# Negative mean, second sum and z on ScalarE, in a two-layer graph network scheduled by a planner

## The chip, the cores and the metric

The kernel runs on one core of one Trainium2 chip. The core has five engines that run side by side, each through its own queue: TensorE (PE in the profile), VectorE (DVE), ScalarE (ACT), GpSimd (POOL) and SyncE (SP), which here only issues DMAs. What is measured is device time in microseconds (us) of one launch; less is better.

## The reference, cut to what matters

There are 64 batches of 256 tokens with 512 features (float32). The first layer is masked attention with 8 heads, the second a graph attention with scores from two vectors; each is added to its input and normalized over the features, without scale or shift.

```python
def _layernorm(x, axis=-1, eps=1e-5):
    m = jnp.mean(x, axis=axis, keepdims=True)
    v = jnp.var(x, axis=axis, keepdims=True)
    return (x - m) / jnp.sqrt(v + eps)

# layer 0: out = softmax(q k^T / 8 + (1 - adj) * -1e9) v, per head
x = _layernorm(x + out @ Wo + bo)
# layer 1
h = x @ W
e = leaky_relu(s1[:, :, None] + s2[:, None, :], 0.2) * adj     # s1 = h a1, s2 = h a2
x = _layernorm(x + elu(softmax(e, axis=2) @ h + beta * h))
```

## The kernel before, in words

**Tiling.** A batch's tokens lie on the 128 partitions in two tiles (NT = 2), with 512 features along the free dimension. Two batches make a pair (function pair, L620): they share the products for q, k and v. There are 32 pairs, m = 0 to 31; the two batches of a pair are s = 0 and s = 1. Every product with a weight is done by project (L435), a seven-product scheme in place of eight: each product goes into a PSUM tile, some are copied out by ScalarE (L495 and, with a bias for q and k, L498) and others added on by VectorE (L504, L954). The copies matter for order: the fourth product of a project adds onto the PSUM tile of the first, so it has to wait until ScalarE has copied the first out; likewise the fifth or sixth (into ps_cross) waits for the copy of the second.

**Steps of a batch.** scores (four products in pairs of heads, L782), mask and exponential (L789, L791), sums (denominators, L805), mix (attention times v, L749), o (output product added to X, L954), the first norm, two dot products of X with vectors on VectorE (L977), logits (the graph scores, L987 to L1028), attention (transposed through DRAM, L1030 to L1050), spread (attention times X, L1106), u (times W, L1111), finish (L716: ELU and the second norm, and the output's DMA).

**norm (L584).** For two tiles of X it takes the sum of each (ScalarE, Identity with an accumulator output; L592), multiplies it by -1/512 on VectorE (mean, L598), squares X plus this negative mean on ScalarE with a sum (L592 again), takes a power of -1/2 on GpSimd (L603 to L605), and applies scale and bias on ScalarE (L609). For the second norm the sum of X comes with the last VectorE operation of finish (L724, accum_out), and is given to norm, which then leaves out its Identity.

**z (L1006).** The graph score of a query and a key is a sum of one number per partition (sv) and one per column (row). The column's numbers are a row that is written to DRAM (line, L1001) and read back to all partitions (row, L1003); z is row plus sv on VectorE. After it come leaky relu (VectorE, L1012), the mask (GpSimd, L1015), the maximum (VectorE, L1017), the exponential (ScalarE, L1020), the division (VectorE, L1026).

**The planner (class Plan, L62).** Every operation is entered with its engine, an assumed duration in ns, what it reads and writes, and a mode. place (L127) simulates the engines with these durations and writes out one order, in which the instructions are issued; each engine then goes through its instructions in that order. An operation of GpSimd, and one of VectorE with the mode "two", takes a common "port" in this simulation and has to wait for it. Of the operations that could start, the one with the earliest start is placed; at equal start the engine that comes first in the table LAG (L73). The lag of each engine is the assumed time until another engine sees its result.

TensorE's operations have a fixed order: take_turn (L613) gives each step of pair m the round m + LATER[step], and inside a round the place in ROUND. The last pairs follow FINISH instead, and for the last 70 TensorE operations (OPEN) the plan chooses freely. "x", "logits" and "attention" are turns without TensorE work: they only fix when their buffers are claimed and what may start after them.

Of the kernel before, what the change touches and what calls it, by code (L numbers as in the profile page):

```python
# [11 lines left out]
AF = mybir.ActivationFunctionType  # L12
ALU = mybir.AluOpType
# [6 lines left out]
ALPHA = 0.2  # L20
NEG = -1000000000.0

ROUND = ("x", "v", "spread1", "scores20", "scores10", "scores30", "scores00", "o1", "q", "logits1", "u1", "sums0",
         "mix0", "scores11", "scores21", "scores01", "scores31", "attention0", "k", "spread0", "o0", "mix1",
         "logits0", "sums1", "u0", "attention1")

LATER = {"scores20": 0, "x": -1, "scores10": 0, "v": 0, "logits0": 0, "spread1": 2, "o1": 1, "q": -1, "u1": 2,
         "sums0": 0, "mix0": 0, "scores11": 0, "scores01": 0, "attention0": 1, "attention1": 1, "scores31": 0,
         "scores21": 0, "k": -1, "logits1": 1, "spread0": 1, "o0": 0, "u0": 1, "sums1": 0, "mix1": 0, "scores00": 0,
         "scores30": 0}  # L30

FINISH = (("scores00", 0), ("scores20", 0), ("scores10", 0), ("v", 0), ("attention1", 1), ("spread1", 2),
          ("scores30", 0), ("logits1", 1), ("o1", 1), ("sums0", 0), ("u1", 2), ("attention0", 1), ("mix0", 0),
          ("scores11", 0), ("spread0", 1), ("u1", 0), ("logits0", 0), ("o0", 0), ("sums1", 0), ("spread1", 1),
          ("mix1", 0), ("attention1", 0), ("spread0", 0), ("scores21", 0), ("attention0", 0), ("u0", 0),
          ("logits1", 0), ("o1", 0), ("u1", 1), ("scores31", 0), ("u0", 1), ("scores01", 0), ("spread1", 0))
SAFE = 1e15


# [22 lines left out]
class Plan:  # L62
# [7 lines left out]

    LAG = {"PE": 260.0, "DVE": 70.0, "ACT": 70.0, "POOL": 90.0, "SP": 4200.0}  # L73
    KEPT = {"PE": 0.0, "DVE": 80.0, "ACT": 95.0, "POOL": 40.0, "SP": 0.0}
    AFTER = {"PE": 0.0, "DVE": 30.0, "ACT": 30.0, "POOL": 80.0}
    SWITCH = {None: 100.0, "rows": 200.0, "columns": 100.0, "sums": 100.0, "one": 100.0}
    AGAIN = 100.0
    LATER = 15000.0
    OPEN = 70
# [47 lines left out]
    def place(self):  # L127
# [22 lines left out]
        for n, o in enumerate(ops):  # L150
            if due[n] is None:
                due[n] = max((due[d] + (self.LATER if ops[d][0] == "PE" else ops[d][1]) for d in o[3]), default=0.0)

# [90 lines left out]
def gnn_two_layers(ctx: ExitStack, tc: tile.TileContext, x, adj, Wq, bq, Wk, bk, Wv, bv, Wo, bo, W, a, beta, out):  # L244
    nc = tc.nc
    B, N, D = x.shape
# [24 lines left out]
    plan = Plan(slots)  # L271
    stay = []
    A = slice(None)
# [7 lines left out]
    def st(n, name):  # L281
        return sb("st", [n], name)
# [298 lines left out]
    for sv in spare:  # L581
        plan.op("POOL", 100, lambda sv=sv: nc.gpsimd.memset(sv[A], 0.0), [], [sv])

    def norm(X, ts, given=None):  # L584

        n = len(ts)
        mean, sq, rs, nm = (st(n, name) for name in ("mean", "sq", "rs", "nmr"))
        sums = given or st(n, "sum")

        def total(i, t, func, to, bias):  # L590
            junk = sb("half", [D], "junk")
            plan.op("ACT", 815 if bias else 725, lambda: nc.scalar.activation(  # L592
                junk[A], X[:, t, :], func, bias=mean[:, i:i + 1] if bias else 0.0, accum_out=to[:, i:i + 1]),
                [(X, (t, 0)), (X, (t, 1))] + ([mean] if bias else []), [junk, (to, i)])

        for i, t in enumerate(ts if given is None else ()):
            total(i, t, AF.Identity, sums, False)
        plan.op("DVE", 170, lambda: nc.vector.tensor_scalar(mean[A], sums[A], -1.0 / D, None, ALU.mult), [sums], [mean])  # L598
        for i, t in enumerate(ts):
            total(i, t, AF.Square, sq, True)  # L600

        def rsqrt():
            nc.gpsimd.tensor_scalar(rs[A], sq[A], 1.0 / D, EPS, ALU.mult, ALU.add)  # L603
            nc.gpsimd.tensor_tensor(rs[A], rs[A], neg_half[A].to_broadcast([P, n]), ALU.pow)
            nc.gpsimd.tensor_tensor(nm[A], mean[A], rs[A], ALU.mult)  # L605

        plan.op("POOL", 1250, rsqrt, [sq, mean], [rs, nm])
        for i, t in enumerate(ts):
            plan.op("ACT", 810, lambda i=i, t=t: nc.scalar.activation(  # L609
                X[:, t, :], X[:, t, :], AF.Identity, bias=nm[:, i:i + 1], scale=rs[:, i:i + 1]),  # L610
                [nm, rs], [(X, (t, 0)), (X, (t, 1))])

    def take_turn(m, what):  # L613
        at_end = (what, B // 2 - 1 - m) if m is not None else None
        if at_end in FINISH:
            plan.turn = (B // 2 + 1, FINISH.index(at_end))
        else:
            plan.turn = ((m or 0) + LATER[what], ROUND.index(what))

    def pair(m, at, general=False):  # L620
# [56 lines left out]
        if m == 0:  # L677
# [11 lines left out]
            left["v"] = weight_sums(wv_sb, "sv_sb", "POOL")  # L689
            plan.turn = (0, ROUND.index("x"))  # L690
            left["o"] = residual_bias()
# [11 lines left out]
    def batch(m, s, qT, kT, V, dram, general):  # L703
# [4 lines left out]
        X = sb("x", [NT, D], f"x_{b}")  # L708
# [4 lines left out]
        def tokens(t):  # L713
            return [(X, (t, 0)), (X, (t, 1))]

        def finish(ts, us, u, mode):  # L716

            sums = st(len(ts), "sum")
            for t in ts:
                m = sb("half", [D], "m")  # L720
                plan.op("ACT", 620, lambda t=t, m=m: nc.scalar.activation(m[A], u(t), AF.Exp), us(t), [m])
                plan.op("DVE", 685, lambda t=t: nc.vector.scalar_tensor_tensor(  # L722
                    X[:, t, :], u(t), 0.0, X[:, t, :], op0=ALU.max, op1=ALU.add), us(t), tokens(t), mode=mode)
                plan.op("DVE", 770, lambda t=t, m=m: nc.vector.scalar_tensor_tensor(  # L724
                    X[:, t, :], m[A], 1.0, X[:, t, :], op0=ALU.min, op1=ALU.add,
                    accum_out=sums[:, t - ts[0]:t - ts[0] + 1]), [m], tokens(t) + [(sums, t - ts[0])], mode="two")
            norm(X, ts, sums)
            for t in ts:
                plan.op("SP", 455, lambda t=t: nc.sync.dma_start(dram(out, s)[:, t, :], X[:, t, :]), tokens(t), [],
                        lag=2300)  # L730
# [238 lines left out]
        if b == 0:  # L969
            plan.turn = (0, ROUND.index("k"))  # L970
            left["w"] = second_layer_constants()

        sv = spare[(b or 0) % len(spare)]
        for t in range(NT):
            for i in range(2):
                junk = sb("half", [D], "junk")
                plan.op("DVE", 770, lambda t=t, i=i, junk=junk: nc.vector.scalar_tensor_tensor(  # L977
                    junk[A], X[:, t, :], 1.0, wa_sb[:, i, :], op0=ALU.mult, op1=ALU.mult,
                    accum_out=sv[:, t, 1 - i:2 - i]), tokens(t) + [(wa_sb, i)], [junk, (sv, (i, t))],
                    mode="two")  # L980


        z, e = sb("half", [NT, N], "z"), sb("half", [NT, N], "e")
# [4 lines left out]
        if near:  # L988
            row = ps([N], "tr_s")
# [6 lines left out]
        else:  # L996
            line, row = Buf(dram_pool, "line", [N], "line"), sb("half", [N], "row")
# [5 lines left out]
            plan.op("SP", 430, lambda: nc.sync.dma_start(row[A], row_on_all(line[A], 0, N)), [line], [row], lag=3800)  # L1003
        nm1, sm1, rc1 = st(NT, "nm1"), st(NT, "sm1"), st(NT, "rc1")
        for t in range(NT):
            plan.op("DVE", 430, lambda t=t: nc.vector.tensor_scalar(  # L1006
                z[:, t, :], row[A], sv[:, t, 1:2], None, ALU.add), [row, (sv, (0, t))], [(z, t)], mode="two")

        for ts in ((0, 1), (1, 2)) if near else ((0, 2),):
            ts, k = slice(*ts), ts[1] - ts[0]  # L1010
# [71 lines left out]
        sums = [(lambda i=i: S[:, i]) for i in range(4)]  # L1082
# [39 lines left out]
    fine, row, least = st(2, "fine"), ps([P], "row"), st(1, "least")  # L1122
# [17 lines left out]
    with tc.If(again != 0):  # L1140
# [3 lines left out]
        with tc.For_i(0, B, 2) as i:  # L1144
            for tile_ in stay:
                tile_.parts = {}
            plan = Plan({**slots, "half": slots["half"] - 1})
# [34 lines left out]
```

## Time and profile before

| what | us |
|---|---|
| median of 3 runs | 2713.54 (2713.28 to 2713.59) |
| the profiled execution, own time | 2716.73 |
| its span, first to last instruction | 2714.9 |
| a round in the middle, from one mix0 to the next | 83.70 |
| PE busy, in that round | 82.25 |
| DVE, ACT, POOL busy in that round | 70.1, 44.6, 51.9 |
| the last PE product to the end of the span | 12.2 |

The profiled execution is 0.12% above the median, so sums over its trace are compared with 2716.73, and the difference is carried over to the median. The busy time of TensorE rests on modelled ends, but a gap between its products is a gap. Between 100 and 2590 us the rounds repeat. The clock of TensorE is full except for 3.5 us near 2641 us.

### The profile page before, as it was taken

How to read it: one execution, taken by the hardware profiler on the slowest of the kernel's cores; microseconds unless marked ns; L12 is line 12 of the kernel's file. 1: busy time of each engine (PE TensorE's matmuls, PEld its weight loads, DVE VectorE, ACT ScalarE, POOL GpSimd, SP SyncE). 2: the span in 40 equal slices, each digit the busy share in tenths (PEclk: the TensorE clock that was granted, in tenths of full speed). 3: DMA queues.
4: the chain of work that ended last, by engine and by line, in shares of the span. 5: the costliest groups of instructions: out<-in, count | busy, mean ns of one | idle time of the engine just before them, and what ended most of it. 6: DMA issues, size and time to landing. Idle time of an engine off the chain costs nothing.

```text
span 2714.9 us, 45841 instructions
## 1 busy us (share of the span) xinstructions
PE 2650.2 (98%) x15037; PEld 2283.0 (84%) x15037; DVE 2256.1 (83%) x4439; ACT 1427.2 (53%) x3201; POOL 1663.8 (61%) x2255
## 2 busy tenths in 40 slices
PE   9999999999999999999999999999999999999997
PEld 7888888888888888888888888888888888888886
DVE  6888888888888888988889888888888888888977
ACT  3455555555554555545555555555455554555555
POOL 5665575655666656656557565575665666656654
PEclk9999999999999999999999999999999999999999
DMA  8444353443444443434435344343444443443321
GB/s 252 95 103 121 101 128 90 116 112 108 121 107 107 106 120 109 122 93 114 119 103 133 86 114 119 105 124 97 116 106 114 115 114 101 108 124 100 98 57 55
DMA packets 583084, 300.70 MB, mean 111 GB/s; under 512 B 409400, under 2 KB 513848, under 8 KB 582840
## 3 DMA queue, kind: packets, MB, share of 16 engines
q1 hardware_dynamic: 582712, 297.68, 41.8%
q8 instruction: 123, 2.02, 0.3%
q14 instruction: 121, 0.99, 0.1%
q0 software_dynamic: 128, 0.01, 0.0%
HBM read 245.11 MB, written 52.48 MB: 110 GB/s over the span
## 4 chain that ended last, share of the span: by engine, by line
PE 87%; DVE 9%; ACT 3%; issue 1%; DMA 0%; POOL 0%; SPq 0%; DVEq 0%; POOLq 0%; ACTq 0%
PE ps_chain L455 29%; PE ps_cross L455 21%; PE ps_sc L782 8%; PE ps_pv L759 8%; PE ps_fourth L455 7%; PE ps_pair L455 7%; PE ps_second L455 5%; DVE mean L598 3%; DVE flip L800 2%; ACT junk L592 2%; DVE part L801 1%; DVE x L954 1%; ACT qT L498 1%; DMA wq_sb<-in_L_gnn_Wq_dram 0%; PE ps_den L809 0%
## 5 line engine op out<-in xcount | busy, mean ns | idle before, releaser
L794 POOL TENSOR_TENSOR both<-pT 128x256 f32<-128x256 f32 x504 | 379.3, 776 | 11.0 <-ACT pT L791 11.0
L791 ACT ACTIVATE pT<-pT 128x512 f32<-128x512 f32 x512 | 309.9, 629 | 106.0 <-DVE pT L789 105.5
L789 DVE TENSOR_TENSOR pT<-ps_sc,maskT_sb 128x512 f32<-128x512 f32 x512 | 317.8, 682 | 13.6 <-PE ps_sc L782 11.6
L1086 POOL TENSOR_TENSOR X_sums<-x 128x256 f32<-128x256 f32 x126 | 126.3, 1018 | 256.2 <-DVE x L722 204.9
L977 DVE SCALAR_TENSOR_TENSOR junk<-x,wa_sb 128x512 f32<-128x512 f32 x256 | 225.1, 914 | 50.6 <-ACT x L609 49.6
L1015 POOL TENSOR_TENSOR e<-e,adj_sb 128x512 f32<-128x512 f32 (+1 forms) x66 | 82.6, 1252 | 290.0 <-DVE e L1012 287.6
L592 ACT ACTIVATE junk<-x 128x512 f32<-128x512 f32 x128 | 80.1, 626 | 322.9 <-DVE x L954 313.7
L592 ACT ACTIVATE junk<-x,mean 128x512 f32<-128x512 f32 x256 | 182.8, 716 | 120.5 <-DVE mean L598 120.5
L782 PE MATMUL ps_sc<-qT,kT 64*128 64x256 f32 x2048 | 238.9, 383 | 0.0
L759 PE MATMUL ps_pv<-pT,v 128*64 128x256 f32 x2048 | 238.4, 382 | 0.0
L609 ACT ACTIVATE x<-x,nmr,rs 128x512 f32<-128x512 f32 x256 | 197.6, 808 | 58.2 <-POOL nmr L605 55.6
L782 PEld LDWEIGHTS ps_sc<-qT,kT 64*128 64x128 f32 x2048 | 192.6, 187 | 37.0 <-issue 13.3
L759 PEld LDWEIGHTS ps_pv<-pT,v 128*64 128x64 f32 x2048 | 175.6, 137 | 44.6 <-issue 11.0
L603 POOL TENSOR_SCALAR rs<-sq 128x2 f32<-128x2 f32 (+1 forms) x130 | 34.8, 268 | 281.9 <-ACT junk L592 276.7
L800 DVE STREAM_TRANSPOSE flip<-both 128x512 f32<-128x512 f32 x252 | 176.6, 701 | 8.2 <-DVE part L801 0.5
L801 DVE TENSOR_REDUCE part<-flip 128x16 f32<-128x512 f32 x252 | 168.8, 670 | 0.3
L455 PE MATMUL ps_cross<-xT,wq_sums 128*128 128x256 f32 x496 | 120.2, 385 | 43.0 <-ACT qT L498 43.0
L743 POOL TENSOR_TENSOR x<-x,res_sb 128x512 f32<-128x512 f32 x128 | 161.0, 1280 | 0.9 <-DMA x<-in_x_dram 0.9
L455 PEld LDWEIGHTS ps_cross<-xT,wq_sums 128*128 128x128 f32 x496 | 91.8, 190 | 65.9 <-ACT qT L498 54.6
L598 DVE TENSOR_SCALAR mean<-sum 128x2 f32<-128x2 f32 (+1 forms) x130 | 112.0, 862 | 34.8 <-ACT junk L592 34.6
L954 DVE TENSOR_TENSOR x<-x,ps_chain 128x256 f32<-128x256 f32 x252 | 101.5, 413 | 40.2 <-PE ps_chain L455 37.0
L455 PE MATMUL ps_chain<-so_sb,oS 128*128 128x256 f32 x504 | 129.7, 380 | 0.0
(248 smaller groups left out, 7179.8 us busy)
## 6 DMA issues: line engine op xcount, KB each, us to landing
x<-in_x_dram SPq DMA_DIRECT2D x64, 512.0 KB, 7.9
out_dram<-x SPq DMA_DIRECT2D x128, 256.0 KB, 3.1
inv_all<-rows SPq DMA_DIRECT2D x126, 256.0 KB, 3.8
xin<-in_x_dram SPq DMA_DIRECT2D x248, 128.0 KB, 3.0
wq_sums<-wq_sums SPq DMA_DIRECT2D x124, 256.0 KB, 3.1
wk_sums<-wk_sums SPq DMA_DIRECT2D x124, 256.0 KB, 2.7
wq_sums<-in_L_gnn_Wq_dram SPq DMA_DIRECT2D x93, 256.0 KB, 2.8
wk_sums<-in_L_gnn_Wk_dram SPq DMA_DIRECT2D x93, 256.0 KB, 3.5
```

Of the source, the lines that this page charges most:

```text
L455: nc.tensor.matmul(dst[:, f, :], lhs, rhs, start=start and f == 0 and c == 0, stop=c == inner - 1, skip_group_check=True)
L592: plan.op("ACT", 815 if bias else 725, lambda: nc.scalar.activation(junk[A], X[:, t, :], func, bias=mean[:, i:i + 1] if bias else 0.0, acc ...
L598: plan.op("DVE", 170, lambda: nc.vector.tensor_scalar(mean[A], sums[A], -1.0 / D, None, ALU.mult), [sums], [mean])
L609: plan.op("ACT", 810, lambda i=i, t=t: nc.scalar.activation(X[:, t, :], X[:, t, :], AF.Identity, bias=nm[:, i:i + 1], scale=rs[:, i:i + 1] ...
L759: nc.tensor.matmul(acc[r * HD:(r + 1) * HD, i, :], V[:, 2 * k + s, h * HD:(h + 1) * HD], pT[h][:, k, :], start=k == 0, stop=k == NT - 1)
L782: nc.tensor.matmul(acc[j][:, k, :], kT[r:r + HD, c, key_blk(k)], own(qT, r, c), start=True, stop=True)
L789: plan.op("DVE", 680, lambda h=h, i=i: nc.vector.tensor_add(pT[h][A], acc[i][A], maskT_sb[A]), [acc[i], maskT_sb], [pT[h]])
L791: plan.op("ACT", 620, lambda h=h: nc.scalar.activation(pT[h][A], pT[h][A], AF.Exp, scale=1.0 / HD ** 0.5), [pT[h]], [pT[h]])
L794: plan.op("POOL", 735, lambda h=h, i=i: nc.gpsimd.tensor_tensor(both[c][:, i, :], pT[h][:, 0, :], pT[h][:, 1, :], ALU.add), [pT[h]], [(bot ...
L800: plan.op("DVE", 700, lambda: nc.vector.transpose(turned[A], both[c][A]), [both[c]], [turned])
L801: plan.op("DVE", 685, lambda: nc.vector.tensor_reduce(part[:, 2 * c:2 * c + 2, :], turned[A].rearrange("p i (q k) -> p i q k", k=32), AX.X ...
L977: plan.op("DVE", 770, lambda t=t, i=i, junk=junk: nc.vector.scalar_tensor_tensor(junk[A], X[:, t, :], 1.0, wa_sb[:, i, :], op0=ALU.mult, o ...
```

## The change

The sum in norm becomes a scaled one: the Identity on ScalarE gets scale -1/512, so that its accumulator output is the negative mean itself, and the VectorE multiplication (L598) is gone. Each Square then depends on the mean of its own tile alone. The second norm does the same: finish no longer has an accumulator output on its last VectorE operation, and norm runs its Identities there too. z moves from VectorE to ScalarE, as an Identity whose bias is sv. In the planner's table of lags GpSimd comes before VectorE now, which decides ties. ROUND, LATER and FINISH are replaced.

```diff
-    LAG = {"PE": 260.0, "DVE": 70.0, "ACT": 70.0, "POOL": 90.0, "SP": 4200.0}
+    LAG = {"PE": 260.0, "POOL": 90.0, "DVE": 70.0, "ACT": 70.0, "SP": 4200.0}
...
-    def norm(X, ts, given=None):
+    def norm(X, ts):
...
-        sums = given or st(n, "sum")
...
-        for i, t in enumerate(ts if given is None else ()):
-            total(i, t, AF.Identity, sums, False)
-        plan.op("DVE", 170, lambda: nc.vector.tensor_scalar(mean[A], sums[A], -1.0 / D, None, ALU.mult), [sums], [mean])
         for i, t in enumerate(ts):
-            total(i, t, AF.Square, sq, True)
+            total(i, t, 725, AF.Identity, mean, scale=-1.0 / D)
+        for i, t in enumerate(ts):
+            total(i, t, 815, AF.Square, sq, bias=lambda i=i: mean[:, i:i + 1])
...
-                plan.op("DVE", 770, lambda t=t, m=m: nc.vector.scalar_tensor_tensor(
-                    X[:, t, :], m[A], 1.0, X[:, t, :], op0=ALU.min, op1=ALU.add,
-                    accum_out=sums[:, t - ts[0]:t - ts[0] + 1]), [m], tokens(t) + [(sums, t - ts[0])], mode="two")
-            norm(X, ts, sums)
+                plan.op("DVE", 685, lambda t=t, m=m: nc.vector.scalar_tensor_tensor(
+                    X[:, t, :], m[A], 1.0, X[:, t, :], op0=ALU.min, op1=ALU.add), [m], tokens(t), mode="two")
+            norm(X, ts)
...
-            plan.op("DVE", 430, lambda t=t: nc.vector.tensor_scalar(
-                z[:, t, :], row[A], sv[:, t, 1:2], None, ALU.add), [row, (sv, (0, t))], [(z, t)], mode="two")
+            plan.op("ACT", 475, lambda t=t: nc.scalar.activation(
+                z[:, t, :], row[A], AF.Identity, bias=sv[:, t, 1:2]), [row, (sv, (0, t))], [(z, t)])
```

The orders, of which only the places that differ in a round are shown: ROUND begins with v, x instead of x, v; the scores of s = 0 come as 20, 00, 10, 30 instead of 20, 10, 30, 00; logits0 moves from after mix1 (with LATER 0) to between o1 and q (with LATER 1).

```diff
-ROUND = ("x", "v", "spread1", "scores20", "scores10", "scores30", "scores00", "o1", "q", "logits1", "u1", "sums0",
-         "mix0", "scores11", "scores21", "scores01", "scores31", "attention0", "k", "spread0", "o0", "mix1",
-         "logits0", "sums1", "u0", "attention1")
+ROUND = ("v", "x", "spread1", "scores20", "scores00", "scores10", "scores30", "o1", "logits0", "q", "logits1", "u1",
+         "sums0", "mix0", "scores11", "scores21", "scores01", "scores31", "attention0", "k", "spread0", "o0", "mix1",
+         "sums1", "u0", "attention1")
...
-FINISH = (("scores00", 0), ("scores20", 0), ("scores10", 0), ("v", 0), ("attention1", 1), ("spread1", 2),
-          ("scores30", 0), ("logits1", 1), ("o1", 1), ("sums0", 0), ("u1", 2), ("attention0", 1), ("mix0", 0),
+FINISH = (("scores20", 0), ("scores30", 0), ("logits0", 1), ("v", 0), ("spread1", 2), ("scores10", 0),
+          ("attention0", 1), ("scores00", 0), ("u1", 2), ("o1", 1), ("sums0", 0), ("scores21", 0), ("mix0", 0),
```

## The prediction

> **What bounds the kernel now.** I read the page's header first: TensorE is busy for 98% of the span, so only PE's gaps (64.7 us in all) can be won unless PE's own work changes.
>
> ```profile
> span 2714.9 us, 45841 instructions
> PE 2650.2 (98%) x15037; PEld 2283.0 (84%) x15037; DVE 2256.1 (83%) x4439; ACT 1427.2 (53%) x3201; POOL 1663.8 (61%) x2255
> PE 87%; DVE 9%; ACT 3%; issue 1%; DMA 0%; POOL 0%; SPq 0%; DVEq 0%; POOLq 0%; ACTq 0%
> ```
>
> The third line, from the chain that ended last, says that 9% of it is DVE nevertheless. So I asked who waited for whom (engine and line, releaser: us in total, times, longest).
>
> ```profile
> PE ps_cross L455 <- ACT qT L498: 43.0, 29, 1.8
> ACT junk L592 <- DVE mean L598: 120.5, 61, 3.4
> ```
>
> Of PE's 64.7 idle us, 43.0 are one wait, met 29 times, 1.48 us each: once per pair. Then two whole rounds by windows (start:end, length, PE, PEld, DVE, ACT, POOL busy, clock, DMA share, GB/s).
>
> ```profile
> 1218.60:1302.30 83.70, 82.24 (x471) 71.11 (x473) 70.25 (x139) 44.56 (x100) 51.78 (x70) 1.00 0.43 111
> 1302.30:1386.00 83.70, 82.25 (x471) 71.12 (x473) 70.06 (x139) 44.55 (x100) 51.87 (x70) 1.00 0.43 111
> ```
>
> A round takes 83.70 us, of which PE is idle 1.45: nothing else is lost in it. Where that comes from, the timeline shows engine by engine (start us, us, engine, line, idle before it and releaser).
>
> ```profile
> 1368.38 1.28 POOL L1015 TENSOR_TENSOR e<-e,adj_sb 128x512 f32<-128x512 f32 x1
> 1369.62 2.49 POOL L743 TENSOR_TENSOR x<-x,res_sb 128x512 f32<-128x512 f32 x2
> 1368.94 3.19 DVE L598 TENSOR_SCALAR mean<-sum 128x2 f32<-128x2 f32 x1
> 1372.17 0.72 ACT L592 ACTIVATE junk<-x,mean 128x512 f32<-128x512 f32 x1 [3.08 <-DVE mean L598]
> 1372.89 0.45 ACT L498 ACTIVATE qT<-ps_cross,bq_sb 128x256 f32<-128x256 f32 x1
> 1373.95 0.46 ACT L498 ACTIVATE qT<-ps_cross,bq_sb 128x256 f32<-128x256 f32 x1
> 1374.46 1.99 PE L455 MATMUL ps_cross<-xT,wq_sums 128*128 128x256 f32 x8 [1.45 <-ACT qT L498]
> ```
>
> The mean of the first norm, two numbers per partition, lasts 3.19 us: exactly as long as GpSimd's three operations need to end (1372.1). ScalarE's Square waits 3.08 us for it, two PSUM copies of q stand behind the Square, and TensorE waits 1.45 us for the second. The product before them ended near 1369.5, so they could have run then.
>
> ```profile
> L598 DVE TENSOR_SCALAR mean<-sum 128x2 f32<-128x2 f32 (+1 forms) x130 | 112.0, 862 | 34.8 <-ACT junk L592 34.6
> L592 ACT ACTIVATE junk<-x 128x512 f32<-128x512 f32 x128 | 80.1, 626 | 322.9 <-DVE x L954 313.7
> L1006 DVE TENSOR_SCALAR z<-row,s 128x256 f32<-128x256 f32 x124 | 54.8, 463 | 0.0
> ```
>
> The mean's median is 170 ns by its line's answer, its average 862 ns: the difference is waiting. The planner books it at 170 and without the mode "two", so it doesn't know that this operation can be held up.
>
> **What the skill says.** "SBUF — State Buffer", section "Who interferes with whom": a VectorE tensor_scalar can enter a 2-port mode, and then takes a port pair shared with GpSimd, exclusively, for the whole instruction; whoever issues first holds it. The 3.19 us agree, though GpSimd kept it over three operations. The same section says that PE and ACT never wait for it: ScalarE's Identity here lasts 612 to 634 ns in all its 128 uses, which agrees. "TensorE: Matmul & The Clock Gate", specifications, calls ScalarE's queue strict FIFO: the q copies behind the Square agree. "ScalarE: Activation LUTs", "What ACT_TABLE_LOAD costs": 280 + 0.833 ns per element with a per-partition bias, so by estimate 493 ns for z on 256 elements; the trace has 500 (L1020, SBUF, same size, bias from a tile).
>
> **The change, part by part.**
>
> Mean by ScalarE. Removed: 130 VectorE operations, 112.0 us, and the hop ScalarE-VectorE-ScalarE. Added for the first norm: nothing but a scale constant in the Identity that is there. Whether a Square must wait for the accumulator read of its own engine the trace doesn't show: between 0 and 0.19 us (that read's own length, L592). I take 0: with two tiles the other Identity lies between. At the stall this means: second Identity done at 1368.4, two chain copies of q until 1369.1, two Squares (0.9 each with the read) until 1370.8, q's cross copies until 1371.6, while PE wants them at 1373.0 (1374.46 - 1.45). Slack 1.4 us; the stall goes wholly: 29 x 1.48 = **-43.0 us**. If this cover is eaten, each us beyond it is 29 us.
>
> The second norm's sum. Added on ScalarE: 128 Identities with read, 0.62 us from start to start (1331.57, 1332.19): 2.5 us a round. Removed on VectorE: 128 accumulator reads (9.9 us in all). It lies behind the final x and in front of the output's DMA only, whose tiles have four slots. On SP's queue that DMA stands later by some 1.3 us, and what is behind it with it: in the round shown (1311.94) fetches of q's weights, needed 50 us on, and the next x. Cost 0 in the rounds, bounds 0 and rival B. Only at the very end it is bare: the last Square starts at 2705.94, when ScalarE is free from three normalizations, so the last Identity adds 0.62 us, bounds 0 and 0.8: **+0.6**.
>
> z by ScalarE. Removed on VectorE 128 x 0.46 = 59 us, port waits among them; added on ScalarE some 0.4 us each from start to start, 1.6 a round. Together ScalarE gets 4.1 us a round onto 44.55: 58% of an 82.2 us round. z adds no hop: VectorE reads it as before; but ScalarE's queue now waits for the row DMA where VectorE's did. No wait before z shows today (0.0 in its line). I take 0; upper bound: rival D.
>
> Planner, ties for GpSimd and LAG's order: no instructions. It moves VectorE operations behind GpSimd's, on engines that PE doesn't wait for in the rounds; 0, bounds -0.2 and +0.2 us a round by judgement (port waits of L977, 0.2 us mean over its 0.69, are the like of it).
>
> Orders. I sorted both lists by (pair + LATER, place in ROUND). TensorE's real work comes in the same order in the rounds: v, spread1, four scores, o1, q, u1, sums0, mix0, four scores, k, spread0, o0, mix1, sums1, u0; only the four scores swap among themselves. So mode switches and PE's 82.25 us stay. What moves are empty turns: x(m+1) goes behind v, and logits0 from after mix1 to just before q of the next round. That moves the svT transpose, the line and row DMAs on SP's queue (0.57 and 0.33 us of issue), z and the softmax later. Attention of that batch must be ready at spread0: by the trace, about 1405 - 1366 = 39 us after o1. Its chain: line and row 7 us, z to division 7, square, att_b and transpose 10, sums 2: 26. Slack 13; cost 0, bounds 0 and, if SP's queue holds it longer, what exceeds 13.
>
> FINISH. From 2596.7 PE is idle 1.69 + 0.23 + 1.71 us and runs 3.5 us at clock 0.51 (1.75 lost). A new order can win at most 5.4; the last 70 products are placed freely by the plan, so the written order doesn't tell. I take **-1.0**, bounds -5 and +5.
>
> Sum against the profiled execution's own time: 2716.7 (span 2714.9 and 1.8 around it) - 43.0 + 0.6 - 1.0 = 2673.3. The median of the runs is 3.2 lower than that execution, so **2670**.
>
> **The rivals.** A, the forecast, 2670; with up to 0.3 us a round left and FINISH at its bounds, 2664 to 2682.
>
> B, part is given back: ScalarE is fuller, and yT's copies are tight. A first product of spread ended at 1322.2, its copy ran 1322.38 to 1322.75, and PE wanted it at 1323.08: 0.33 us spare. A Square (0.81 to the next start) that has just begun delays PE by some 0.5. Two spreads a round, two such copies each: one or two of the four hit give 0.5 to 1.0 us a round, 15 to 29 us: 2685 to 2699. Against it: the plan knows these durations and serves the most urgent first.
>
> C, the change doesn't do it: the Identity itself waits for VectorE's last addition (L954 is its releaser for 313.7 us), and if the additions come 3 us later, q's copies stay as late as now: 2713. Against it: those additions end at 1367.6, and neither they nor the flips and reductions among them show port waits.
>
> D, slower: the wait is replaced by z's. Logits0 stands now just before q. If z is at the head of ScalarE's queue when the row DMA is just issued, it waits 4.0 us (its landing time), with q's copies behind it. Today's ScalarE wait of 3.08 us cost 1.45, so the projection absorbs 1.6; PE would stand 2.4 us instead of 1.48: +0.9 x 29 = 27 us, **2741**. It decides from a wait of 1.6 + 1.48 + 0.18 = 3.3 us. For it: SP's issues of this chain wait up to 2.3 us for VectorE today. Against it: z started 5.8 and 6.6 us after the row's issue in the rounds shown, and the plan books 4.2 from issue to arrival.
>
> **How the numbers follow.** A 0.66, B 0.14, C 0.06, D 0.14. A measurement can tell about 0.2% (5.4 us) from no change. Faster is A and B, 0.80; same C, 0.06; slower D, 0.14. The range leaves out D, C and little of A: 2664 to 2700.
>
> **What would show it.** Right: PE's wait for qT L498 gone from the list, a round near 82.25 us, no mean on VectorE, 256 Identities with a read on ScalarE, ScalarE near 1590 us busy, VectorE near 2080. B would show as waits of PE for yT; D as idle time of ScalarE in front of z with the row DMA as releaser; C as a longer wait of the Identity for L954. A round of 83.7 us or more makes the forecast wrong.

## The result, and the profile after

The changed kernel takes **2666.81 us** (median of 4 runs, 2666.57 to 2668.14); the kernel before, on the same chip, 2713.57 (2713.28 to 2715.03). The ratio is 0.983 (95% interval 0.981 to 0.985). The forecast was 2670, the range 2664 to 2700. The profiled execution of the changed kernel took 2666.57, with a span of 2664.8.

The header of its page, and the chain that ended last, by engine:

```profile
span 2664.8 us, 45965 instructions
PE 2643.7 (99%) x15037; PEld 2288.5 (86%) x15037; DVE 1999.7 (75%) x4053; ACT 1550.5 (58%) x3585; POOL 1637.5 (61%) x2255
PE 98%; DVE 0%; ACT 0%; DMA 0%; SPq 0%; issue 0%; POOL 0%; ACTq 0%; DVEq 0%
```

VectorE has left the chain (9% before). These are all the waits of TensorE that the trace lists (engine and line, releaser: us in total, times, longest):

```profile
PE tr_x L642 <- DMA xin<-in_x_dram: 4.6, 2, 3.8
PE ps_cross L455 <- POOL oT L425: 2.2, 1, 2.2
PE ps_chain L455 <- DVE wq_sums_s L387: 0.7, 1, 0.7
PE ps_chain L455 <- DVE oT L873: 0.6, 1, 0.6
PE ps_chain L455 <- ACT yT L495: 0.2, 1, 0.2
```

The wait for qT, 43.0 us in 29 pieces, is gone, and no wait that comes back every round stands in its place. Two rounds by windows (start:end, length, PE, PEld, DVE, ACT, POOL busy, clock, DMA share, GB/s):

```profile
1280.00:1361.98 81.98, 81.98 (x469) 71.30 (x468) 62.13 (x128) 48.32 (x112) 50.90 (x70) 1.00 0.43 113
1361.98:1443.96 81.98, 81.98 (x469) 71.29 (x468) 62.22 (x128) 48.40 (x112) 50.95 (x70) 1.00 0.42 113
```

TensorE is busy in all of the 81.98 us. The timeline of ScalarE, GpSimd and TensorE at the place of the old stall (start us, us, engine, line, idle before it and releaser):

```profile
1348.14 0.63 ACT L591 ACTIVATE junk<-x 128x512 f32<-128x512 f32 x1 [3.85 <-DVE x L951]
1348.53 2.52 POOL L740 TENSOR_TENSOR x<-x,res_sb 128x512 f32<-128x512 f32 x2
1349.12 0.62 ACT L591 ACTIVATE junk<-x 128x512 f32<-128x512 f32 x1
1350.11 0.47 ACT L498 ACTIVATE qT<-ps_cross,bq_sb 128x256 f32<-128x256 f32 x1
1350.48 0.71 ACT L591 ACTIVATE junk<-x,mean 128x512 f32<-128x512 f32 x1
1351.19 0.46 ACT L498 ACTIVATE qT<-ps_cross,bq_sb 128x256 f32<-128x256 f32 x1
1353.36 1.89 PE L455 MATMUL ps_cross<-xT,wq_sums 128*128 128x256 f32 x8
```

The Identity now leaves the negative mean itself, the Square follows on the same engine without a wait although GpSimd is at work, and the second cross copy of q is done near 1351.65. TensorE comes to it at 1353.36: 1.7 us of slack where it had to wait 1.48.

**Where the 50.1 us of the two spans lie.** I cut both traces at the first product of k, which occurs once a round (ps_chain from xT and the sums of Wk, 31 times in each).

| stretch | before | after | difference |
|---|---|---|---|
| start to the second of them | 137.13 | 142.29 | +5.2 |
| 29 rounds (83.73, 81.98 each) | 2428.24 | 2377.53 | -50.7 |
| the last of them to the end | 149.53 | 144.98 | -4.5 |
| span | 2714.9 | 2664.8 | -50.1 |

The medians differ by 46.8, since the profiled execution of before lies 3.2 above its median, and that of after 0.2 below.

### The profile page after: what moved, and what is told of

Its sections match the earlier page's. It is cut to its first block, busy times and chain, and to the rows that moved or that the text cites. A ratio compares the mean times of both kernels' runs of the same rounds, so it can differ in the third digit from the quotient of the medians.

```text
span 2664.8 us, 45965 instructions
## 1 busy us (share of the span) xinstructions
PE 2643.7 (99%) x15037; PEld 2288.5 (86%) x15037; DVE 1999.7 (75%) x4053; ACT 1550.5 (58%) x3585; POOL 1637.5 (61%) x2255
## 4 chain that ended last, share of the span: by engine, by line
PE 98%; DVE 0%; ACT 0%; DMA 0%; SPq 0%; issue 0%; POOL 0%; ACTq 0%; DVEq 0%
PE ps_chain L455 35%; PE ps_cross L455 23%; PE ps_sc L779 9%; PE ps_pv L756 9%; PE ps_pair L455 8%; PE ps_fourth L455 7%; PE ps_second L455 7%; PE ps_den L806 0%; DMA wq_sb<-in_L_gnn_Wq_dram 0%; ACT junk L591 0%; PE ps_plain L523 0%; DVE wq_sums_s L387 0%; DVE oT L873 0%; PE ps_y L1058 0%; PE ps_plain L518 0%; PE ps_plain L520 0%
## 5 line engine op out<-in xcount | busy, mean ns | idle before, releaser
L791 POOL TENSOR_TENSOR both<-pT 128x256 f32<-128x256 f32 x504 | 361.3, 742 | 55.9 <-ACT pT L788 55.8
L602 POOL TENSOR_SCALAR rs<-sq 128x2 f32<-128x2 f32 (+1 forms) x130 | 25.4, 195 | 537.5 <-ACT junk L591 534.6
L591 ACT ACTIVATE junk<-x 128x512 f32<-128x512 f32 x256 | 159.7, 624 | 330.1 <-DVE x L951 311.8
L974 DVE SCALAR_TENSOR_TENSOR junk<-x,wa_sb 128x512 f32<-128x512 f32 x256 | 173.9, 691 | 46.7 <-ACT x L608 46.6
L740 POOL TENSOR_TENSOR x<-x,res_sb 128x512 f32<-128x512 f32 x128 | 160.8, 1278 | 0.9 <-DMA x<-in_x_dram 0.9
L455 PE MATMUL ps_chain<-sw_sb,yS 128*128 128x256 f32 x504 | 129.4, 379 | 0.0
L455 PE MATMUL ps_chain<-sv_sb,xS 128*128 128x256 f32 x512 | 120.9, 379 | 0.0
L425 POOL TENSOR_TENSOR oS<-oT 128x256 f32<-128x256 f32 x126 | 101.2, 803 | 30.8 <-DVE oT L873 23.1
L455 PE MATMUL ps_chain<-xS,wk_sums 128*128 128x256 f32 x496 | 117.2, 379 | 0.0
```

The lines of the kernel that those rows point to most:

```text
L455: nc.tensor.matmul(dst[:, f, :], lhs, rhs, start=start and f == 0 and c == 0, stop=c == inner - 1, skip_group_check=True)
L591: plan.op("ACT", ns, lambda: nc.scalar.activation(junk[A], X[:, t, :], func, accum_out=to[:, i:i + 1], **{k: v() if callable(v) else v for ...
L740: plan.op("POOL", 1300, lambda t=t: nc.gpsimd.tensor_tensor(X[:, t, :], X[:, t, :], res_sb[A], ALU.add), [res_sb], tokens(t))
L791: plan.op("POOL", 735, lambda h=h, i=i: nc.gpsimd.tensor_tensor(both[c][:, i, :], pT[h][:, 0, :], pT[h][:, 1, :], ALU.add), [pT[h]], [(bot ...
```

## The experiments

The theory: the mean, two numbers per partition on VectorE, was held up by GpSimd, and ScalarE with q's copies behind it; taking it out of that place gives the whole gain of the rounds. Rivals: the new orders did it; the relief of VectorE did it (z and the second sum); any VectorE mean is too late there, port or not. Two side questions: what the last pairs gained, and what the head lost. The ratios are to runs of before on the same chip (its medians there were 2713.57 to 2714.71). "First round" and "end" are the stretches from the first to the second product named above, and from the last one on, each in one profiled execution; where two kernels share a stretch of the plan they agree in it within 0.1 us (first round of before, e1, e2, e3; end of after, e8, e10), except where the clock differs (last section).

| kernel | median us | ratio (95%) | round | first round | end |
|---|---|---|---|---|---|
| before | 2713.57 | 1 | 83.73 | 63.55 | 149.5 |
| after | 2666.81 | 0.9811 to 0.9845 | 81.98 | 68.69 | 145.0 |
| e1 before, mean by a reduction | 2663.51 | 0.9800 to 0.9833 | 81.98 | 63.55 | 147.6 |
| e2 before, first mean by ScalarE | 2670.17 | 0.9823 to 0.9856 | 81.98 | 63.54 | 153.1 |
| e3 before, the plan knows the port | 2674.84 | 0.9839 to 0.9869 | 81.98 | 63.55 | 157.9 |
| e7 before, new orders | 2699.81 | 0.9930 to 0.9963 | 82.92 | 64.93 | 154.6 |
| e11 e1, mean 2.7 us later | 2707.75 | 0.9967 to 0.9985 | 83.38 | 64.17 | 150.5 |
| e9 after, both means on VectorE | 2671.56 | 0.9826 to 0.9856 | 81.98 | 68.71 | 149.9 |
| e4 after, old orders | 2669.90 | 0.9824 to 0.9857 | 81.98 | 66.53 | 149.9 |
| e5 after, z on VectorE | 2672.49 | 0.9830 to 0.9860 | 81.98 | 68.70 | 152.0 |
| e6 after, old ties | 2671.95 | 0.9831 to 0.9858 | 81.98 | 64.92 | 150.8 |
| e8 after, residual's product first | 2666.01 | 0.9808 to 0.9834 | 81.98 | 69.76 | 145.0 |
| e10 after, old ties in the head | 2663.05 | 0.9797 to 0.9823 | 81.98 | 64.87 | 144.9 |

### e1: a mean on VectorE that GpSimd cannot hold up

Only the kind of the operation changes, and the factor -1/512 goes into the Identity before it; all engines keep the order of before. "SBUF — State Buffer", section "Who interferes with whom", says that tensor_reduce never contends with GpSimd on trn2. Here it takes 136 ns on average over 65 uses, 158 at most.

```diff
...
+                scale=1.0 if bias else -1.0 / D, accum_out=to[:, i:i + 1]),
...
-        plan.op("DVE", 170, lambda: nc.vector.tensor_scalar(mean[A], sums[A], -1.0 / D, None, ALU.mult), [sums], [mean])
+        if given is None:
+            plan.op("DVE", 170, lambda: nc.vector.tensor_reduce(
+                mean[A], sums[A].unsqueeze(2), AX.X, ALU.add), [sums], [mean])
+        else:
+            plan.op("DVE", 170, lambda: nc.vector.tensor_scalar(
+                mean[A], sums[A], -1.0 / D, None, ALU.mult), [sums], [mean])
```

> The kernel before with its order of instructions on every engine unchanged; only the first norm's mean is another VectorE instruction: the scale -1/512 goes into the Identity, and the mean is a tensor_reduce over one element in place of a tensor_scalar. The hop from ScalarE to VectorE and back stays. Theory (the shared port holds the tensor_scalar up, and with it ScalarE's queue and q's copies): the mean lasts about 0.2 us always, PE's wait for qT goes, the round falls from 83.7 to about 82.0 us, and the time by 29 x 1.74 = 50 us to about 2663. Rival 1 (the hop itself, or VectorE's load, is what costs): about 2713. Rival 2 (the new orders make the gain): about 2713.

Measured: 2663.51 us, rounds of 81.98. The timeline of e1 around the mean:

```profile
1339.54 3.48 POOL L800 TENSOR_TENSOR both<-pT 128x256 f32<-128x256 f32 x5
1342.98 1.27 POOL L1021 TENSOR_TENSOR e<-e,adj_sb 128x512 f32<-128x512 f32 x1
1343.53 0.11 DVE L600 TENSOR_REDUCE mean<-sum 128x2 f32<-128x2 f32 x1
1343.67 0.72 ACT L592 ACTIVATE junk<-x,mean 128x512 f32<-128x512 f32 x1
1344.22 2.50 POOL L749 TENSOR_TENSOR x<-x,res_sb 128x512 f32<-128x512 f32 x2
```

GpSimd's run is the same as before, mask multiply and residual back to back; the mean goes through the middle of it in 0.11 us, and the Square starts at once. So the hold-up of this one instruction is the whole loss of the rounds: one operation of another kind, on the same engine and in the same order, brings as much there as the change does. The whole of e1 takes 2663.51 us against 2666.81; that it is quicker is not shown, since the intervals of the two ratios overlap.

### e11: the same mean, late for another reason

Four reductions over 512 elements, whose results nothing uses, stand before e1's mean of one batch of each pair; the plan knows nothing of them.

```diff
+            def late_mean():
+                for _ in range(4 if slow else 0):
+                    nc.vector.tensor_reduce(scrap[A], X[:, 0, :], AX.X, ALU.add)
+                nc.vector.tensor_reduce(mean[A], sums[A].unsqueeze(2), AX.X, ALU.add)
...
```

> The port-free mean (first experiment), with four reductions over 512 elements put ahead of it for the second batch of each pair, unknown to the plan; their results are not used. They take VectorE some 0.6 us each and no port. It tells whether the lateness of the mean is what costs, by whatever it comes. Theory: a mean that is late by about 2.4 us holds the Square and the copies of q behind it; the projection absorbs some 1.5 us of ScalarE's wait, so PE waits about 0.8 to 1.3 us for qT in each round, a round takes 82.9 to 83.5 us, and the time is 2690 to 2712. Rival (the port as such slows ScalarE or PE, not the lateness): rounds of 82.0, about 2664.

Measured: 2707.75 us, rounds of 83.38. The timeline of e11:

```profile
1281.54 2.81 DVE L604 TENSOR_REDUCE scrap<-x 128x1 f32<-128x512 f32 x4
1284.27 0.14 DVE L605 TENSOR_REDUCE mean<-sum 128x2 f32<-128x2 f32 x1
1284.45 0.72 ACT L594 ACTIVATE junk<-x,mean 128x512 f32<-128x512 f32 x1 [2.76 <-DVE mean L605]
1286.74 1.99 PE L455 MATMUL ps_cross<-xT,wq_sums 128*128 128x256 f32 x8 [1.13 <-ACT qT L498]
```

The stall is back, by lateness alone: ScalarE waits 2.76 us, TensorE 1.13. Of ScalarE's wait the projection absorbs 1.63 here, 1.63 before (3.08 - 1.45). A gap of 1.13 costs a round 1.40 us (83.38 - 81.98), not 1.13.

### e2: only the first norm's mean on ScalarE

```diff
...
+                scale=1.0 if bias else -1.0 / D, accum_out=to[:, i:i + 1]),
...
-            total(i, t, AF.Identity, sums, False)
-        plan.op("DVE", 170, lambda: nc.vector.tensor_scalar(mean[A], sums[A], -1.0 / D, None, ALU.mult), [sums], [mean])
+            total(i, t, AF.Identity, mean, False)
+        if given is not None:
+            plan.op("DVE", 170, lambda: nc.vector.tensor_scalar(
+                mean[A], sums[A], -1.0 / D, None, ALU.mult), [sums], [mean])
```

> The kernel before with only the first norm's mean moved to ScalarE as the scaled sum; the second norm, z, ties and orders as before. The plan is made anew, as one VectorE operation is gone. Theory: no wait of PE for qT, about 2663 (2658 to 2672 as the plan shifts other things). Rival 1 (VectorE's load, of which the second mean and z are a part): some half of the gain, 2680 to 2700. Rival 2 (orders): about 2713.

Measured: 2670.17 us; the rounds are at 81.98, so the second sum, z, ties and orders add nothing to them. The first round is before's, the end 3.6 us longer: new waits of TensorE there (1.95 us for a dot product, six more below 1).

### e3: nothing moved, but the plan knows

```diff
-        plan.op("DVE", 170, lambda: nc.vector.tensor_scalar(mean[A], sums[A], -1.0 / D, None, ALU.mult), [sums], [mean])
+        plan.op("DVE", 170, lambda: nc.vector.tensor_scalar(mean[A], sums[A], -1.0 / D, None, ALU.mult), [sums], [mean],
+                mode="two")
```

> The kernel before with one word more in the plan: the mean on VectorE has the mode "two", so that the plan lets it wait for the port and books the wait; the same instructions, placed anew. Theory (the loss comes from a wait that the plan doesn't know): knowing it, the plan puts GpSimd's or q's operations otherwise and a part or all of the wait goes: rounds of 82.0 to 83.0 us, 2663 to 2693. Rival (the wait is there wherever a mean on VectorE stands): rounds of 83.7, about 2713.

Measured: 2674.84 us. The same 130 VectorE means, now 158 ns on average (862 before), and rounds of 81.98: once the plan books the port for it, the mean no longer meets GpSimd's run. The end is 8.4 us longer than before's; its longest waits of TensorE there are 2.3, 2.1, 1.9 and 1.3 us.

### e7: the new orders alone

ROUND, LATER and FINISH of after, everything else of before.

> The kernel before with the new ROUND, LATER and FINISH alone; mean and z stay on VectorE. Theory: the mean is still an operation that the plan books at 170 ns and the port can hold up, so some wait stays, of a size that depends on what GpSimd does there: 2690 to 2730. Rival 2 (the orders make the gain): 2662 to 2675.

Measured: 2699.81 us, rounds of 82.92. The wait for qT is gone in the rounds, but another has come. The timeline of e7:

```profile
1367.75 1.75 DVE L977 SCALAR_TENSOR_TENSOR junk<-x,wa_sb 128x512 f32<-128x512 f32 x1
1368.91 2.30 POOL L1086 TENSOR_TENSOR X_sums<-x 128x256 f32<-128x256 f32 x2
1371.89 0.66 DVE L1017 TENSOR_REDUCE nm<-e 128x2 f32<-128x512 f32 x1
1372.59 0.51 ACT L1020 ACTIVATE e<-e,nm 128x256 f32<-128x256 f32 x1 [1.93 <-DVE nm L1017]
1373.10 0.35 ACT L495 COPY u<-ps_cross 128x256 f32<-128x256 f32 x1
1373.50 1.13 PE L455 MATMUL ps_cross<-sw_sb,yT 128*128 128x256 f32 x4 [0.67 <-ACT u L495]
```

A dot product on VectorE takes 1.75 us beside GpSimd's work, the next one 1.20 (0.68 when alone); the maximum stands behind them in VectorE's queue and is late, the exponential waits 1.93 us at the head of ScalarE's queue, a copy of u stands behind it, and TensorE waits 0.67 us, 29 times. It is the old stall's pattern with other operations; that the dot products are what makes the maximum late is read from the timeline, and no run takes them away. So the orders explain part of the gain only if the mean stays on VectorE, and none beyond e2's.

### e9: both means back on VectorE, in the changed kernel

```diff
+        sums = st(n, "sum")
...
-            total(i, t, 725, AF.Identity, mean, scale=-1.0 / D)
+            total(i, t, 725, AF.Identity, sums)
+        plan.op("DVE", 170, lambda: nc.vector.tensor_scalar(mean[A], sums[A], -1.0 / D, None, ALU.mult), [sums], [mean])
```

> The changed kernel with one part undone: both means are VectorE's again (an unscaled sum on ScalarE, then the multiplication on VectorE, booked at 170 ns and without the port); z, second sum, ties and orders stay changed. Theory: GpSimd works without a pause where the first norm's mean would stand, so it is held up again by 1 to 3 us and PE waits for a copy of ScalarE in each round: rounds of 82.5 to 84 us, 2680 to 2720. Rival 1 (VectorE's load is what costs): rounds stay 82.0 and the time 2667 to 2671.

Measured: 2671.56 us. This expectation was missed: no stall in the rounds. It is what the rival there, VectorE's load, forecast, but e1 speaks against that: it takes no operation off VectorE and has no stall either. The timeline of e9:

```profile
1348.82 2.54 POOL L742 TENSOR_TENSOR x<-x,res_sb 128x512 f32<-128x512 f32 x2
1350.52 0.86 DVE L599 TENSOR_SCALAR mean<-sum 128x2 f32<-128x2 f32 x1
1351.42 0.72 ACT L592 ACTIVATE junk<-x,mean 128x512 f32<-128x512 f32 x1 [0.54 <-DVE mean L599]
```

The mean is still held until GpSimd's run ends (1351.36), but the mask multiply no longer lies in that run. The mean takes 0.86 us in place of 0.17, ScalarE waits 0.54, and that is less than the 1.6 that the projection absorbs. In the changed kernel there are thus two cures for one stall, the mean on ScalarE and the other place of the mask multiply, each enough by itself (e4, e9); what one of them is worth is only seen where the other is absent: e2 has the one, e7 the other, with a new gap in its place.

### e4: the changed kernel with the old orders

ROUND, LATER and FINISH of before, everything else of after.

> The changed kernel with the ROUND, LATER and FINISH of before. Theory: the rounds keep 82.0 us, since TensorE's order is the same and the mean is on ScalarE; without the new FINISH about 5 us of the end come back, without the head's loss 5 us go: 2662 to 2672. Rival 2 (the orders make the gain): a stall of 0.5 us or more a round returns, above 2681.

Measured: 2669.90 us, rounds of 81.98. The end takes 149.9 against 145.0, so in this kernel the new orders are worth about 5 us there. They are not worth that by themselves: e7 has them too, and its end is 5 us longer than before's (154.6 against 149.5). The first round takes 66.5 against 68.7, so the new orders cost 2.2 there. Of this 1.7 is the clock: in after TensorE runs at half clock for 3.4 us there, in e4 it doesn't, although it waits 2.72 us for oT.

### e5: z back on VectorE

```diff
-            plan.op("ACT", 475, lambda t=t: nc.scalar.activation(
-                z[:, t, :], row[A], AF.Identity, bias=sv[:, t, 1:2]), [row, (sv, (0, t))], [(z, t)])
+            plan.op("DVE", 430, lambda t=t: nc.vector.tensor_scalar(
+                z[:, t, :], row[A], sv[:, t, 1:2], None, ALU.add), [row, (sv, (0, t))], [(z, t)], mode="two")
```

> The changed kernel with z on VectorE again, as a "two" operation. Theory: in the rounds PE waits for nothing, so z's place is worth nothing there: 81.98 us a round; the plan of the end shifts, 2665 to 2675. If z's move is part of the gain: a wait of PE in each round, above 2681.

Measured: 2672.49 us. Rounds and first round stand as in after: z on ScalarE is worth 0 there. The end is 7 us longer.

### e6, e8, e10: what the head lost

In the changed kernel TensorE waits 0.56 and 2.21 us for oT in the first round. The timeline of after there:

```profile
83.11 3.15 DVE L873 TENSOR_TENSOR oT<-oT,inv_all 128x512 f32<-128x512 f32 x1
83.23 1.26 POOL L740 TENSOR_TENSOR x<-x,res_sb 128x512 f32<-128x512 f32 x1
84.45 1.27 POOL L375 TENSOR_TENSOR sw_sb<-w_sb 128x512 f32<-128x512 f32 x1
86.41 1.10 PE L455 MATMUL ps_chain<-wo_sb,oT 128*128 128x256 f32 x4 [0.56 <-DVE oT L873]
89.72 2.00 PE L455 MATMUL ps_cross<-wo_sb,oT 128*128 128x256 f32 x4 [2.21 <-POOL oT L425]
91.52 1.89 PE L455 MATMUL ps_pair<-wo_sb,oT 128*128 128x256 f32 x4
```

Here it is VectorE's product of oT that is held, 3.15 us instead of 0.68. In the kernel before, the two of them stand together, ahead of the flips and reductions and 5.8 us earlier (its timeline):

```profile
77.35 2.18 DVE L876 TENSOR_TENSOR oT<-oT,inv_all 128x512 f32<-128x512 f32 x2
86.54 1.03 PE L455 MATMUL ps_cross<-wo_sb,oT 128*128 128x256 f32 x4
```

e8 moves the product for the residual's bias (ps_b, L546) back ahead of v, where it stood before; e6 and e10 give ties to VectorE again, e6 throughout, e10 in the plan's first 95 us.

```diff
# e8
-            plan.turn = (0, ROUND.index("x"))
+            plan.turn = (0, -1)
# e6
-    LAG = {"PE": 260.0, "POOL": 90.0, "DVE": 70.0, "ACT": 70.0, "SP": 4200.0}
+    LAG = {"PE": 260.0, "DVE": 70.0, "ACT": 70.0, "POOL": 90.0, "SP": 4200.0}
# e10
+    FIRST = ("PE", "DVE", "ACT", "POOL", "SP")
+    HEAD = 95000.0
...
-            for e, cand in ready.items():
+            for e in self.FIRST if now["PE"] < self.HEAD else self.LAG:
+                cand = ready[e]
```

> The changed kernel with the table of lags in the order of before, so that VectorE takes the port in ties. Theory: the rounds stay at 81.98 us; only the first pair and the end move, 2660 to 2675, and VectorE's port waits come back in part (the dot products L974, 691 ns on average in the changed kernel, 914 before). If the ties carry the gain, a wait of PE in each round returns: above 2680.

Measured: 2671.95 us. The first round is 3.8 us shorter (64.92), as it should be if ties are the cause; but the second is 84.02 (two waits, of 0.74 us for kT and 0.79 for yT), and the end 5.8 us longer.

> The changed kernel with the product for the residual bias put ahead of v in the first round, where it stood before; ROUND's swap of x and v had moved it behind v. If that late place makes the first round's loss (PE waits 0.56 and 2.21 us for oT at 86 to 90 us, and is slow after it; the first round is 68.7 us, before 63.6), the time falls by some 5 us to about 2662. If the tie rule makes it (the product of oT with the inverse sums lasts 3.15 us beside GpSimd), nothing changes: 2666 to 2668.

Measured: 2666.01 us; the first round is 69.76, with a wait of 2.38 us for oT. The product stands at 35.8 us instead of 47.6, and the wait stays, so its late place is not the cause. GpSimd goes through its operations in the same order as in after, the residual's additions (L740) among them: their place was not tested.

> The changed kernel with ties given to VectorE for the plan's first 95 us only, and to GpSimd afterwards. If the tie rule makes the first round's loss (5 us against the kernel before, by the wait of oT behind GpSimd's run of residual and weight sums), the first round falls from 68.7 to 64 or 65 us and the time to 2662 to 2664, unless the plan's end shifts. If not: 2666 to 2668.

Measured: 2663.05 us (2662.44 to 2663.22). The timeline of e10:

```profile
82.57 2.23 DVE L876 TENSOR_TENSOR oT<-oT,inv_all 128x512 f32<-128x512 f32 x2
87.58 1.13 PE L458 MATMUL ps_cross<-wo_sb,oT 128*128 128x256 f32 x4 [0.51 <-POOL oT L428]
```

Both products take 2.23 us, TensorE waits 0.51 instead of 2.21, the first round is 64.87, and rounds and end stay as in after. The tie rule caused 3.8 of the head's 5.2 us. This version has the lowest median of all, though e1's (2663.51) is not told apart from it. Its runs lie below all of after's (2666.57 at the least), by 3.8 us in the median, with before at 2714.70 beside it and at 2713.57 beside after; the intervals of the two ratios to before overlap, and the 3.8 us of the first round are what tells them apart.

## Why the prediction was right

**The bound and the mechanism** were right. The gain lies in the 29 rounds, at the one wait named; e1 shows that GpSimd's hold on the mean is its cause, e11 that lateness is what costs, and e3 that the plan's ignorance left it there.

**Mean by ScalarE, -43.0: right, mis-sized; it measured -50.7.** The wrong term is 1.48 for a stall; it is 1.74 to 1.75. The step "mode switches and PE's 82.25 us stay" hid it: 82.25 of busy time held a part of the stall. Every round with one gap has it, every round without has 81.98:

| kernel | gap of PE us | busy PE in the round | round | round less 81.98 | that less the gap |
|---|---|---|---|---|---|
| before | 1.48 | 82.25 | 83.73 | 1.75 | 0.27 |
| e11 | 1.13 | 82.25 | 83.38 | 1.40 | 0.27 |
| e7 | 0.67 | 82.25 | 82.92 | 0.94 | 0.27 |

The 0.27 can be read from the timelines. Groups of eight products last 1.89 us and start 1.73 apart in an unbroken stream (before: 1292.59, 1294.32, 1296.04), so neighbours overlap by 0.16 in the records; a gap is counted from the modelled end and misses this. The group after the gap takes 1.99 instead of 1.89. 0.16 + 0.10 = 0.26. "Perfetto Trace Analysis", "Tensor Engine Instruction (MATMUL, LD_WEIGHTS)", says that the profiler estimates the end of a product; the overlap agrees.

**The Square's wait for its own engine's read, 0: right at the stall,** where other operations stand between. No wait is listed before it, it follows the copy before it in the queue, and the slack worked out at 1.4 measured 1.7 (1.6 in e2, which keeps the old orders). It is not 0 everywhere: of the 128 Squares in after that come next after an Identity in the queue, 65 start 0.61 us after it and 63 start 0.75 us after it. The last Square of the kernel is of the second kind: it comes right behind the Identity of its own tile (2654.75, 2655.49). So the read then costs some 0.13 us.

**Second norm, z, orders, ties in the rounds, 0: right.** e2 without all of these has the same 81.98, e5 without z as well. z waited for its row once in 124 uses (2.4 us) and took the 500 ns estimated. **The last Identity, +0.6:** from the end of the last weight product (ps_plain) to the end of the span it went from 12.3 to 12.8, +0.5. Other work in this stretch stands in another order too, so that the Identity makes the 0.5 is not shown.

**FINISH, -1.0: mis-sized.** The end measured -5.05 without the last Identity, at the bound given. The idle 1.69 + 0.23 + 1.71 us and the stretch at half clock are gone; one wait of 0.22 is left after 2600. The order is not what is worth this: put into the kernel before (e7), it makes the end 5.1 us longer, and e5, e6 and e9, which keep it, end at 149.9 to 152.0. So -5.05 is how the placement of this one plan came out, and that it came out well is luck as far as these runs tell; of the two bounds, after met -5 and e7 +5.

**Ties, 0: failed in the head,** where I forecast nothing: +5.2. I looked for what the tie rule does in the repeating rounds only. In the first round GpSimd has weight sums and residuals to do; at a tie it now goes first, and the product of oT comes late into a run of them. e10 shows 3.8 of it. The other 1.4 come with the new orders: e7 has them with the old ties, and its first round is as long as e10's (64.93 and 64.87, before 63.55). The two shares are not independent: with the old orders (e4) the first round is 3.0 longer than before's, and in both kernels the waits, 0.27 for each gap and the half clock account for nearly all of the loss, 0.56 + 2.21 + 2 x 0.27 + 1.7 = 5.0 of 5.1 in after, 2.72 + 0.27 = 3.0 of 3.0 in e4.

**The sum:** -50.7 + 5.2 + 0.5 - 5.05 = -50.1 in the spans, where -43.4 was forecast. From 2716.7 this gives 2666.6, and the median is 2666.81. The forecast took off 3.2 more, because before's profiled execution was that far above its median; after's was not above its own. That the forecast lies only 3.2 from the median is in part luck: 7.7 missed in the rounds and 4.0 in the end went one way, 5.2 missed in the head and the 3.2 carried over went the other.

**The rivals.** B did not come: TensorE waits for yT once, 0.2 us, with ScalarE at 48.3 us a round. C did not: the Identity waits in all as long as before for the last addition (311.8 us, 313.7 before), and that was early enough. D did not: no z waits in a round. Its chain did show in e7, with the exponential in z's place: a wait of 1.93 us of an instruction at the head of ScalarE's queue, 0.67 for TensorE. Two sums of the prediction were off: by its own bounds A reaches from 2666 to 2685 (2670 - 4 and 2670 + 8.7 + 6), not from 2664 to 2682, and 48.65 us of 82.2 are 59%, not 58. Busy times: ScalarE was forecast near 1590 and has 1550.5 (its own 4.1 us a round would have given 1558); VectorE near 2080, and has 1999.7. The dot products account for 51 of this: 914 ns each before, 691 after, since GpSimd holds them less (the group after):

```profile
L974 DVE SCALAR_TENSOR_TENSOR junk<-x,wa_sb 128x512 f32<-128x512 f32 x256 | 173.9, 691 | 46.7 <-ACT x L608 46.6
```

e6, with the old ties, has 824 ns: the tie rule takes more than half of this away. In the rounds no one waits for them, so it is worth nothing there.

**What stays open.** The end takes 145 us in after, e8 and e10, and 148 to 158 in the other kernels, e5, e6 and e9 with after's FINISH among them. Any small change of the plan moves it, and a stretch at half clock, worth 1.7 us, falls into some ends (once in before, e2, e5 and e7, twice in e3) and not into others. The waits that appear are told above in part, but which step of the placement makes them was not isolated. So of the medians only what repeats in the rounds, and the first round, is put down to an edit here.

## What to carry to other kernels

When a tiny operation has a mean far above its median, look at what runs beside it, and at whose queue stands behind its reader: two numbers per partition cost this kernel 1.9% of its time. Before moving work, try the cheapest cure, an operation of a kind that isn't held up, or telling the planner of the shared port: here each alone removed the stall. Price a gap of TensorE by the interval of the rounds, not by its listed length, and look at head and end apart from the rounds, since a rule that is harmless in the rounds can cost there.

## What the hardware showed that I had not expected

- A held operation of VectorE can wait through a whole run of GpSimd's back-to-back operations, not one of them: the mean 3.19 us over three, oT's product 3.15 us over two whole and the rest of a third (0.68 alone). It doesn't always: in before, from 1377.6 on, the dot products and GpSimd's sums of X (L1086) take turns, 1.20 and 1.05 to 1.15 us each where 0.68 and 0.72 are usual. What decides between the two was not isolated.
- Half clock after short gaps, but not after all of them. By windows of after (columns as above):

```profile
86.00:89.70 3.70, 1.10 (x4) 0.68 (x4) 3.21 (x7) 0.00 (x0) 2.84 (x3) 1.00 0.27 87
89.70:93.30 3.60, 3.58 (x9) 2.86 (x10) 0.42 (x1) 0.00 (x0) 1.45 (x2) 0.53 0.00 0
```

With TensorE busy for 1.10 us of 3.70, the clock fell to 0.53 in the next 3.6 us, and two groups of four products took 2.00 and 1.89 us instead of 1.03: some 1.8 us on top of waits of 2.8. "TensorE: Matmul & The Clock Gate", "What's actually happening", has the clock follow recent activity, in windows of about 3.4 us. The lengths agree: by windows of 0.1 us every stretch at half clock between the first 15 us and the last product lasts 3.4 us, in after, before, e2, e3, e5, e7 and e9, and in e8 twice that, 6.8. Which gaps cause one is not clear from their length. The single gaps of 1.48 us in the rounds never did (clock 1.00), nor did one of 2.72 in the head of e4. In the end, before and e1 have the same gaps in front of the same products; the timeline of before, then of e1:

```profile
2638.84 0.68 PE L455 MATMUL ps_cross<-attT,X_sums 128*128 128x128 f32 x4 [1.69 <-DVE pT L789]
2639.75 1.23 PE L455 MATMUL ps_chain<-wo_sb,oT 128*128 128x256 f32 x4 [0.23 <-DVE pT L789]
2640.77 1.91 PE L455 MATMUL ps_cross<-wo_sb,oT 128*128 128x256 f32 x4
```

```profile
2587.36 0.68 PE L455 MATMUL ps_cross<-attT,X_sums 128*128 128x128 f32 x4 [1.69 <-DVE pT L795]
2588.27 1.13 PE L455 MATMUL ps_chain<-wo_sb,oT 128*128 128x256 f32 x4 [0.23 <-DVE pT L795]
2589.24 1.03 PE L455 MATMUL ps_cross<-wo_sb,oT 128*128 128x256 f32 x4
```

In before the clock falls, in e1 it stays at 1.00, and e1's end is 1.9 us shorter, of which the clock makes 1.7. So a change can win or lose such a stretch by chance.
- An accumulator read on ScalarE is an instruction of its own, 0.19 us, yet costs its queue next to nothing: from the Identity's start to that of the next instruction it is 0.63 us (1348.14, 1348.77), from the Square's 0.71 (1350.48, 1351.19), their own lengths. The prediction had booked 0.9 for a Square.
